# Summing messages by source: one-hots made one group ahead, and two turns in one PSUM bank

## The chip, the cores and the metric

The kernel runs on one core of a Trainium2 chip. The metric is device time in microseconds (us), from the start of the program to its end. The core has five engines with queues of their own: TensorE (PE, with its weight loads as PEld), VectorE (DVE), ScalarE (ACT), GpSimd (POOL) and SyncE (SP, which here only issues DMA transfers). An instruction starts when its turn in its engine's queue comes and the semaphores that it waits for have been raised.

## The reference

The kernel computes two graph layers and two mixture-of-experts layers on 6250 nodes with 256 features and 100000 edges. Only the first graph layer's sum matters here:

```python
row, col = (edge_index[0], edge_index[1])          # source and target of each edge
deg = segment_sum(ew_sl, row_sl, num_segments=N)
dinv = jnp.where(deg > 0, rsqrt(deg), 0.0)
norm = dinv[row_sl] * ew_sl * dinv[col_sl]
xw = h6_all @ W
msgs = xw[col_sl] * norm[:, None]
h7 = segment_sum(msgs, row_sl, num_segments=N) + b
h = relu(h7 @ W1 + b1)
out = h @ W2 + b2
```

`segment_sum` adds each edge's message to the row of its source node. After it come the two-layer head, a router over 8 experts (top 2), the experts, a second graph layer with 8 relations, and a second expert layer.

## The kernel before, in words

The nodes are held in 49 blocks of 128. A *turn* is a tile of 128 messages that all belong to one block; there are 830 turns (T), padded to 832 (TL), and they are taken in 104 groups of 8.

Before the stage in question, the messages stage (L848 to L935) has made each edge's message with a one-hot matmul (`pxn`, L908), scaled it on ACT (`msgn`, L923) and scattered it by an indirect DMA into the DRAM tensor `msgs`, in order of source. In that stage two message tiles already share one PSUM bank (L905, L906). Each row of `msgs` carries 256 values and the source number.

`sum_messages` (L944 to L972) then does, for each group:

- L948: the block numbers of the 8 turns are read into DVE registers;
- L949, L950: one load of 1 MB, `g`, is issued on SP; the tile has 4 buffers;
- L952: DVE makes `key`, from which each message's row in its block follows;
- L953 to L966: the 8 one-hot matrices `m` (2 buffers) are made: turns 0 and 1 by one DVE instruction (L954), turns 2 and 3 by two ACT instructions each (`far`, L963, then L964), turns 4 to 7 by POOL (L966);
- L967 to L972: for each turn one matmul (f32, which shows as two passes with a weight load each) writes `ps`, half of a PSUM bank, and DVE adds it to the block's place in the accumulator `acc` in SBUF (L971). The place is known only at run time, so each addition has a small register instruction in front of it. `psum_mm` (L67) hands out banks from a pool of 4.

`sum_messages` is a generator. `sum_and_send` (L1254) drives it. After each turn it may take one step of `send_group` (L1136), which for blocks whose sum is complete runs the head (`pt_h7`, `pg2`), the normalisation, the router (`pl1`, the small DVE steps of `route` and `top`) and the scatter of the rows to the experts (`xs`, L1243, on POOL). It also issues eight loads of `fw1` (L1274).

The order in which each engine takes its instructions is not the program's. The framework's scheduler decides it when the kernel is built, places the semaphore waits, and moves instructions that are ready ahead of others; `tc.keep_in_program_order` pins an instruction behind those that the program has before it on its engine. In the kernel before, the scheduler places `key` some three groups ahead of the additions of its group, and `m`'s DVE part one to two groups ahead.

The kernel is built with two versions of the stage, tags `l` and `e`; with these inputs the one tagged `e` runs, and the profile shows its tiles as `g0e`, `m0e`, `pa0e`.

Of the kernel before, what the change touches and what calls it, by code (L numbers as in the profile page):

```python
# [17 lines left out]
ENG = mybir.EngineType  # L18

N = 6250  # L20
D = 256
E = 100000
NT = 49
# [5 lines left out]
T = C_ + NT - 1  # L29
TL = (T + 7) // 8 * 8  # L30
# [27 lines left out]
def gnn_ffn_kernel(ctx: ExitStack, tc: tile.TileContext, a, out):  # L58
    nc = tc.nc
# [7 lines left out]
    def psum_mm(name):  # L67
        return p_mm.tile([128, 512], F32, tag="mm", name=name)
# [81 lines left out]
    col0, n = {}, 0  # L150
# [25 lines left out]
    def blocks_of(blk, t0, engines, top):  # L176
        _, v = nc.values_load_multi_w_load_instructions(
            blk[0:1, t0 : t0 + 8],
            engines=engines,
            min_val=0,  # L180
            max_val=top,
            skip_runtime_bounds_check_because="it is counted or bounded",
        )
        return v
# [176 lines left out]
    with tc.If(unsorted > 0):  # L361
        with tc.tile_pool(name="reorder", bufs=1) as rp:
# [49 lines left out]
            for q in range(QN):  # L412
                n = min(128, C_ - q * 128)
# [52 lines left out]
    for q0 in range(0, QN, 4):  # L466
        n = min(4, QN - q0)
# [53 lines left out]
    for b in range(NT):  # L521
        for h in range(2):
# [4 lines left out]
                start=(b == 0),  # L527
                stop=(b == NT - 1),
# [124 lines left out]
    for c0 in range(0, TN, DCH):  # L653
# [21 lines left out]
        for c in range(DCH):  # L675
# [4 lines left out]
                start=(c0 + c == 0),  # L680
                stop=(c0 + c == TN - 1),
# [30 lines left out]
    for t in range(NT):  # L712
        here = acc[:, t * D : (t + 1) * D]
# [15 lines left out]
    blks = g0p.tile([1, TL], I32, name="blks")  # L729
    firsts = g0p.tile([128, TL], F32, name="firsts")  # L730
# [212 lines left out]

    def sum_messages(pool, tag):  # L944

        for t0 in range(0, TL, 8):
            n = min(8, T - t0)
            blocks = blocks_of(blks, t0, [ENG.DVE], NT)  # L948
            g = pool.tile([128, 8, RW], F32, name=f"g0{tag}_{t0}", tag="g", bufs=4)  # L949
            nc.sync.dma_start(g, by_tile[:, t0 : t0 + 8, :])  # L950
            key = pool.tile([128, 8], F32, name=f"key{tag}{t0}", tag="key")
            nc.vector.tensor_sub(key[:, :n], firsts[:, t0 : t0 + n], g[:, :n, D])  # L952
            m = pool.tile([128, 8, 128], F32, name=f"m0{tag}_{t0}", tag="m", bufs=2)  # L953
            nc.vector.tensor_tensor(  # L954
                m[:, :2],
                minus[:, None, :].to_broadcast([128, 2, 128]),
                key[:, :2, None].to_broadcast([128, 2, 128]),
                OP.is_equal,
            )
            for j in range(2, n):  # L960
                if j < 4:
                    far = pool.tile([128, 128], F32, name=f"far{tag}{t0}_{j}", tag="far", bufs=2)
                    nc.scalar.activation(far, lanes, AF.Abs, bias=key[:, j : j + 1])  # L963
                    nc.scalar.activation(m[:, j], far, AF.Relu, bias=ones[:, 0:1], scale=-1.0)  # L964
                else:
                    nc.gpsimd.tensor_scalar(m[:, j], minus, key[:, j : j + 1], None, op0=OP.is_equal)  # L966
            for j in range(n):  # L967
                ps = psum_mm(f"pa0{tag}_{t0 + j}")
                nc.tensor.matmul(ps[:, :D], m[:, j, :], g[:, j, :D], start=True, stop=True)  # L969
                here = acc[:, bass.ds(blocks[j] * D, D)]  # L970
                nc.vector.tensor_add(here, here, ps[:, :D])  # L971
                yield t0 + j + 1  # L972

    def aggregate(pool, acc, table, tag):
# [279 lines left out]
    def sum_and_send(tag, early):  # L1254


        with (
            tc.tile_pool(name=f"sum{tag}", bufs=3, side="right") as sump,
            tc.tile_pool(name=f"mlp{tag}", bufs=1) as mlp,
        ):  # L1260
            seen, steps, waiting = [], None, list(GROUPS)

            def step(through):
                nonlocal steps
                if steps is None and waiting and through(sum(waiting[0])):
                    g, n = waiting.pop(0)
                    steps = send_group(g, n, mlp, tag, seen)
                if steps is not None and next(steps, steps) is steps:
                    steps = None

            for turn in sum_messages(sump, tag):
                if turn % 8 == 0 and 5 <= turn // 8 < 13:
                    e = turn // 8 - 5
                    nc.sync.dma_start(fw1[:, e], a["L0_ffn_w1"][e].rearrange("(k p) f -> p k f", p=128))  # L1274
                if early:
                    step(lambda blocks: S_TURNS * blocks + S_SLACK <= turn)
            while steps is not None or waiting:
                step(lambda blocks: True)
# [185 lines left out]
    def rows_in(t, i, stats):  # L1464

        xn = work.tile([128, D], F32, name=f"xn2_{t}", tag="xn", bufs=3)
        normed_in(xn, t, i, stats)
        xT = work.tile([128, 2, 128], F32, name=f"xT2_{t}", tag="xT")
        transpose_to(f"x2_{t}", xT, xn)
        return xT  # L1470
# [5 lines left out]
    ready = {0: rows_in(0, 0, stats[0])}  # L1476
    for gi, t, i in tiles:
# [12 lines left out]
        for r in range(0, NR, 2):  # L1490
            ps = psum_mm(f"phx{t}_{r}")
            for k in range(2):
# [4 lines left out]
                    start=(k == 0),  # L1497
                    stop=(k == 1),
# [11 lines left out]
        ps = psum_mm(f"plo{t}")  # L1510
# [219 lines left out]
```

## Time and profile before

| | |
|---|---|
| median of 3 runs | 4390.7 us (4375.65 to 4398.58) |
| the profiled execution's own time | 4087.26 us |
| its span | 4085.5 us |
| mean granted TensorE clock | 0.926 of full |
| PE, DVE, ACT, POOL busy | 85%, 50%, 32%, 55% of the span |
| matmuls of `pa0e` (L969), 2 passes a turn | 1344.7 to 2046.2 us |
| additions (L971) | 830, 0.42 us each |
| matmul rows of L969 | 1660, 501.7 us busy in all |
| POOL's one-hots (L966) | 414 of 0.64 us on the mean |
| ACT's one-hots (L964), second step | 208 of 0.40 us |
| DVE's one-hots (L954) | 104 of 0.42 us |

The profile is of one execution. A row of a group gives its source line, engine, operation, what it writes and reads (`out<-in`), how often, the busy time, the mean of one, and how long the engine stood idle just before and for whom. A row of the timeline gives start, length, engine, line and operation, and in brackets the idle time before it and the instruction whose end ended it. A row of the table by stretches gives the busy time and number of instructions of each engine. "Granted clock" is the share of full speed that TensorE was allowed.

### The profile page before, as it was taken

Reading aid. Unit: us, or ns where it says so; the run is one execution under the profiler, and the core shown is the slowest. Engines: PE = TensorE matmul, PEld = TensorE weight load, DVE = VectorE, ACT = ScalarE, POOL = GpSimd, SP = SyncE. Lnnn points to the kernel's source line nnn. Section 1 sums busy time; section 2 is a strip of 40 time slices with the busy share of each in tenths; the row PEclk is TensorE's granted clock in tenths of the full one; section 3 lists DMA queues with packets and bytes.
Section 4 is the critical chain, followed back from the end, with each engine's and each line's share of the span. In section 5 each row is a group of like instructions: output and inputs, shape, how many; then the busy total and the mean of one; then the engine's idle time right before and its main releaser. Section 6 shows DMA issues by size and latency. Waiting matters only on the chain.

```text
span 4085.5 us, 53140 instructions
## 1 busy us (share of the span) xinstructions
PE 3465.1 (85%) x14649; PEld 2311.2 (57%) x14649; DVE 2036.3 (50%) x5609; ACT 1325.1 (32%) x3006; POOL 2263.1 (55%) x2450
## 2 busy tenths in 40 slices
PE   7968877777776568888879968997789999999999
PEld 5756665665655345555557623443456666666656
DVE  6872111111111347778843387664556666666562
ACT  3714333333333113333334434663112222222213
POOL 1007777777777235555530086334767777777740
PEclk9989889989898679999989989997789999999999
DMA  4434333333333435555543345446555555555530
GB/s 120 168 112 161 128 126 126 129 128 129 127 128 122 150 112 199 198 199 195 182 154 108 99 166 195 197 197 226 151 141 152 154 150 155 150 151 150 148 110 9
DMA packets 227433, 602.86 MB, mean 148 GB/s; under 512 B 40620, under 2 KB 121689, under 8 KB 207276
## 3 DMA queue, kind: packets, MB, share of 16 engines
q0 software_dynamic: 100736, 295.11, 23.2%
q1 hardware_dynamic: 108242, 287.41, 20.9%
q10 hardware_dynamic: 18138, 16.68, 1.2%
q8 instruction: 131, 2.15, 0.2%
q14 instruction: 186, 1.52, 0.1%
HBM read 362.97 MB, written 236.11 MB: 147 GB/s over the span
## 4 chain that ended last, share of the span: by engine, by line
PE 37%; DVE 10%; issue 4%; DMA 2%; ACT 2%; POOL 2%; DVEq 0%; ACTq 0%; POOLq 0%; SPq 0%
PE ph_e1a L246 6%; PE py1a L1075 6%; PE pa1a L996 6%; PE ph_e2a L246 5%; PE phx L1493 4%; PE pf L1412 2%; PE pf L1428 2%; DVE rest L1503 2%; PE pa0e L969 2%; DVE acc L971 1%; DVE acc L1000 1%; DVE hx L1487 1%; PE pt_fh L234 1%; PE pcb1a L1595 1%; PE pqa L1567 1%
## 5 line engine op out<-in xcount | busy, mean ns | idle before, releaser
L988 POOL DMA_INDIRECT g1a<-hx,idxT x830 | 825.1, 994 | 321.0 <-PE pa1a L996 142.9
L908 PE MATMUL pxn<-acc,sTn 128*128 x3128 | 795.2, 415 | 243.4 <-DVE sTn L891 240.5
L926 POOL DMA_INDIRECT msgs<-msgn,at x782 | 785.4, 1004 | 271.0 <-DMA msgs<-msgn,at 122.8
L908 PEld LDWEIGHTS pxn<-acc,sTn 128*128 128x128 f32 x3128 | 618.5, 207 | 419.2 <-DVE sTn L891 272.3
L969 PE MATMUL pa0e<-g0e,m0e 128*128 128x256 f32 x1660 | 501.7, 436 | 156.2 <-DVE acc L971 70.8
L923 ACT ACTIVATE msgn<-pxn,ewT 128x256 f32<-128x256 f32 x782 | 370.2, 473 | 649.9 <-PE pxn L908 495.7
L1000 DVE TENSOR_TENSOR acc<-acc,pa1a 128x256 f32 x830 | 346.5, 417 | 341.2 <-PE pa1a L996 310.9
L969 PEld LDWEIGHTS pa0e<-g0e,m0e 128*128 128x128 f32 x1660 | 292.8, 206 | 328.7 <-issue 127.8
L966 POOL TENSOR_SCALAR m0e<-minus,keye 128x128 f32<-128x128 f32 x414 | 260.0, 642 | 318.8 <-PE pa0e L969 274.8
L899 DVE COPY msgn<-srcT 128x32 f32<-128x32 f32 x98 | 17.9, 185 | 829.6 <-DMA msgs<-msgn,at 666.7
L996 PE MATMUL pa1a<-g1a,m1a 128*128 128x256 bf16 x2490 | 375.5, 283 | 51.4 <-DMA g1a<-hx,idxT 36.1
L996 PEld LDWEIGHTS <-m1a 128*128 128x128 bf16 x2490 | 243.8, 100 | 275.8 <-issue 193.5
L1493 PE MATMUL phx<-wr,xT 128*128 128x512 f32 x784 | 370.1, 616 | 28.6 <-DVE rest L1503 20.8
L971 DVE TENSOR_TENSOR acc<-acc,pa0e 128x256 f32 x830 | 347.1, 418 | 94.7 <-PE pa0e L969 44.8
L1075 PE MATMUL py1a<-w_L_ffn_expert_w,v2a 128*128 128x256 f32 x1176 | 286.5, 384 | 6.0 <-DVE acc L1000 3.0
L246 PE MATMUL ph_e1a<-xT3a,w_L_ffn_expert_w 128*128 128x512 f32 (+2 forms) x672 | 288.5, 556 | 0.0
L246 PE MATMUL ph_e2a<-v1a,w_L_ffn_expert_w 128*128 128x512 f32 (+2 forms) x672 | 280.1, 542 | 2.1 <-DVE acc L1000 1.3
L253 ACT ACTIVATE v1a<-ph_e1a,cols 128x512 f32<-128x512 f32 (+2 forms) x168 | 106.5, 634 | 539.0 <-PE ph_e1a L246 532.0
L1493 PEld LDWEIGHTS phx<-wr,xT 128*128 128x128 f32 x784 | 148.0, 197 | 189.3 <-issue 163.7
L1453 POOL DMA_INDIRECT y<-ys,ats x98 | 97.3, 993 | 275.9 <-issue 261.1
L1075 PEld LDWEIGHTS py1a<-w_L_ffn_expert_w,v2a 128*128 128x128 f32 x1176 | 208.7, 190 | 44.1 <-ACT v2a L253 10.1
L1076 DVE SCALAR_TENSOR_TENSOR X<-py1a,C1a,X 128x256 f32<-128x256 f32 x294 | 138.8, 480 | 112.4 <-PE py1a L1075 111.4
(649 smaller groups left out, 4330.3 us busy)
## 6 DMA issues: line engine op xcount, KB each, us to landing
g0e<-msgs SPq DMA_DIRECT2D x104, 1040.0 KB
hx<-hx SPq DMA_DIRECT2D x49, 1536.0 KB
rowsn<-lane_rows SPq DMA_DIRECT2D x98, 256.0 KB
fx<-xs SPq DMA_DIRECT2D x105, 128.0 KB
ys<-fy ACTq DMA_DIRECT2D x105, 128.0 KB
g1a<-hx,idxT POOLq DMA_INDIRECT x830
msgs<-msgn,at POOLq DMA_INDIRECT x782
msgs<-none SPq DMA_DIRECT2D x10, 650.0 KB
```

Of the source, the lines that this page charges most:

```text
L246: nc.tensor.matmul(ps[:, :ncols], w[:, k, f * 128 : (f + 1) * 128], xT[:, k, :ncols], start=(k == 0), stop=(k == 1),)
L908: nc.tensor.matmul(come, sT[:, k, j, :], acc[:, bass.ds(blocks[j] * D + k * D, D)], start=(k == 0), stop=(k == 1),)
L923: nc.scalar.activation(msg[:, j, :D], come, AF.Copy, scale=ewT[:, t0 + j : t0 + j + 1])
L926: ins = nc.gpsimd.indirect_dma_start(out=msgs, out_offset=bass.IndirectOffsetOnAxis(ap=at[:, t0 + j : t0 + j + 1], axis=0), in_=msg[:, j, ...
L966: nc.gpsimd.tensor_scalar(m[:, j], minus, key[:, j : j + 1], None, op0=OP.is_equal)
L969: nc.tensor.matmul(ps[:, :D], m[:, j, :], g[:, j, :D], start=True, stop=True)
L971: nc.vector.tensor_add(here, here, ps[:, :D])
L988: nc.gpsimd.indirect_dma_start(out=g, out_offset=None, in_=table, in_offset=bass.IndirectOffsetOnAxis(ap=idxT[:, t0 + j : t0 + j + 1], axi ...
L996: nc.tensor.matmul(ps[:, :D], m[:, j, :], g[:, k * D : (k + 1) * D], start=(k == 0), stop=(k == 2))
L1000: nc.vector.tensor_add(here, here, ps[:, :D])
L1075: nc.tensor.matmul(ps[:, :D], hT[:, k, j : j + 128], w[:, k, :], start=(k == 0), stop=(k == 1))
L1493: nc.tensor.matmul(ps, xT[:, k, :], wr[:, k, r : r + 2, :].rearrange("p r o -> p (r o)"), start=(k == 0), stop=(k == 1),)
```

## The change

Three things change in `sum_messages`; nothing else does.

The loads are issued by `take`, three groups before the loop and then one for the group three ahead, at the top of each turn of the loop. The key and the one-hots of a group are made by `one_hots`, which is called once before the loop for group 0, and then inside the loop after the second addition (j == 1) of each group, for the next group. The subtraction that makes the key is pinned with `keep_in_program_order`, so it can't be moved ahead of that second addition on DVE; the one-hots read the key. Third, two neighbouring turns write the two halves of one bank: `pair` is taken for even j, and `ps` is its left or right half.

```diff
-        for t0 in range(0, TL, 8):
-            n = min(8, T - t0)
-            blocks = blocks_of(blks, t0, [ENG.DVE], NT)
+        def take(t0):
             g = pool.tile([128, 8, RW], F32, name=f"g0{tag}_{t0}", tag="g", bufs=4)
             nc.sync.dma_start(g, by_tile[:, t0 : t0 + 8, :])
+            return g
+
+        def one_hots(t0, g):
+            n = min(8, T - t0)
             key = pool.tile([128, 8], F32, name=f"key{tag}{t0}", tag="key")
-            nc.vector.tensor_sub(key[:, :n], firsts[:, t0 : t0 + n], g[:, :n, D])
+            tc.keep_in_program_order(nc.vector.tensor_sub(key[:, :n], firsts[:, t0 : t0 + n], g[:, :n, D]))
             m = pool.tile([128, 8, 128], F32, name=f"m0{tag}_{t0}", tag="m", bufs=2)
...
+            return m
+
+        come = {t0: take(t0) for t0 in (0, 8, 16)}
+        ready = one_hots(0, come[0])
+        for t0 in range(0, TL, 8):
+            n = min(8, T - t0)
+            blocks = blocks_of(blks, t0, [ENG.DVE], NT)
+            if t0 + 24 < TL:
+                come[t0 + 24] = take(t0 + 24)
+            g, m = come.pop(t0), ready
             for j in range(n):
-                ps = psum_mm(f"pa0{tag}_{t0 + j}")
-                nc.tensor.matmul(ps[:, :D], m[:, j, :], g[:, j, :D], start=True, stop=True)
+                if j % 2 == 0:
+                    pair = psum_mm(f"pa0{tag}_{t0 + j}")
+                ps = pair[:, j % 2 * D : (j % 2 + 1) * D]
+                nc.tensor.matmul(ps, m[:, j, :], g[:, j, :D], start=True, stop=True)
                 here = acc[:, bass.ds(blocks[j] * D, D)]
-                nc.vector.tensor_add(here, here, ps[:, :D])
+                nc.vector.tensor_add(here, here, ps)
+                if j == 1 and t0 + 8 < TL:
+                    ready = one_hots(t0 + 8, come[t0 + 8])
                 yield t0 + j + 1
```

Below, "a" and "b" are the first and the second turn of a pair, that is the left and the right half of a bank.

## The prediction

> **What bounds the kernel now.** I read the busy table by slices first (it says where TensorE is busy and at what clock), then the page's row of L969, then the waits inside that stage, then single instructions. The change touches only the sums by source (L944 to L972), which run from the first matmul of `pa0e` at 1344.7 us to the end of the last addition at 2048.2 us: 703.5 us of the span of 4085.5. The split by stretches:
>
> ```profile
> 1344.00:1543.00 199.00, 131.61 (x391) 88.35 (x391) 88.59 (x283) 37.73 (x112) 61.08 (x92) 0.76 0.38 132
> 1543.00:2048.00 505.00, 441.17 (x1854) 290.28 (x1853) 399.54 (x1526) 171.41 (x505) 285.67 (x410) 0.97 0.58 193
> ```
>
> Columns: length, then busy us of PE, PE's weight loads, DVE, ACT and POOL, then the granted clock, DMA share, GB/s. There are two regimes. The additions' own rows by stretch count 158 turns in the first 199 us (1.26 us a turn, 10.1 us for a group of 8) and leave 672 for the other 505 us (0.75 a turn, 6.0 a group). What DVE waits for over the whole stage (total us, times, longest):
>
> ```profile
> DVE keye L952 <- DMA g0e<-msgs: 72.9, 22, 8.5
> DVE acc L971 <- PE pa0e L969: 44.8, 74, 4.0
> DVE m0e L954 <- PE pa0e L969: 33.6, 23, 2.6
> ```
>
> 67.9 of the 72.9 us fall in the first stretch. A key sits in DVE's queue three groups ahead of its additions, so it waits for a load whose buffer only just came free, and the additions behind it wait too:
>
> ```profile
> 1391.27 0.17 DVE L952 TENSOR_TENSOR keye<-firsts,g0e 128x8 f32<-128x8 f32 x1 [3.59 <-DMA g0e<-msgs]
> 1391.44 0.42 DVE L971 TENSOR_TENSOR acc<-acc,pa0e 128x256 f32 x1
> 1391.97 0.30 PEld L969 LDWEIGHTS pa0e<-g0e,m0e 128*128 128x128 f32 x2 [3.87 <-issue]
> 1392.00 0.67 PE L969 MATMUL pa0e<-g0e,m0e 128*128 128x256 f32 x2 [3.50 <-DVE acc L971]
> 1392.36 2.52 DVE L971 TENSOR_TENSOR acc<-acc,pa0e 128x256 f32 x5 [0.50 <-DVE acc L971]
> ```
>
> In the second stretch those waits are gone. Additions follow each other every 0.52 us (five in 2.52), and small DVE steps of the sending hide in the 0.1 us between two. Hardly any slack is left: DVE and PE are each busy about 80 to 87%, and four banks let PE run four turns ahead.
>
> **What the change does, part by part.**
>
> *Keys and loads.* Each key now stands after the second addition of a group, for the next group, and its load was issued three groups ahead. A load lands about 4.9 us after issue (1386.40 to the key at 1391.27) and has some 15 us. The DMA wait goes: at most 72.9 us. SP's order of loads stays.
>
> *One-hots.* `m` uses buffers freed a group earlier, so DVE's 33.6 us of waiting for them goes. In the built order the DVE one-hot stands before the next addition in 22 groups (22 x 0.42 = 9 us on the path), and in a gap that exists anyway in the other 82. ACT's four steps take about 1.4 us (two pairs of 0.69) and POOL's 2.56, against a need about 2 and 4 us after the key: hidden, unless POOL's scatters (about 1 us each) stand ahead. Without that cover a late one-hot blocks all of PE's queue; 22.6 us of such waits are in the second stretch now, and I leave them.
>
> *Two turns in one bank.* This decides. In the built order of the changed kernel PE no longer does turns in sequence. In a quiet group it does (31.0b is the second half of group 31's pair 0)
>
> ```
> PE   31.0b 31.1b 32.0a 32.1a 31.2b 32.2a 31.3b 32.3a 32.0b ...
> DVE  load-of-blocks 31.0a 31.0b KEY 31.1a M 31.1b 31.2a 31.2b 31.3a 31.3b load-of-blocks 32.0a ...
> ```
>
> and every b matmul carries a wait on DVE that nothing but the addition of its own first half explains: already 0.0b has it, when all banks are fresh and its one-hot was there for 0.0a. DVE stays a, b, a, b. So after each first addition DVE stands until PE has filled the other half. The before trace has this hand-off with nothing in between:
>
> ```profile
> 1615.10 0.41 DVE L971 TENSOR_TENSOR acc<-acc,pa0e 128x256 f32 x1
> ...
> 1615.63 0.30 PEld L969 LDWEIGHTS pa0e<-g0e,m0e 128*128 128x128 f32 x2 [0.49 <-issue]
> 1615.66 0.67 PE L969 MATMUL pa0e<-g0e,m0e 128*128 128x256 f32 x2 [0.23 <-DVE seene L1215]
> ...
> 1616.33 0.42 DVE L971 TENSOR_TENSOR acc<-acc,pa0e 128x256 f32 x1 [0.65 <-DVE placee L1229]
> ```
>
> Addition ends 1615.51, weights start 1615.63 (0.12), the waiting addition starts 1616.33 (0.70). A pair's round is therefore 0.12 + 0.70 + 0.42 (b added) + 0.10 + 0.42 (next a added) = 1.76 us, against two turns at 0.75 = 1.50 now. The a half that PE does meanwhile starts 0.12 after b's addition and streams 0.43: it is out of the way by 0.58, the next b is due at 0.64. At full clock it hides with 0.06 to spare. Behind a waiting b in PE's queue stand the next a and, where sending runs, its transposes (ACT's copies wait for them); behind the waiting addition on DVE stand all later additions, the next key (ACT and POOL wait for it) and the sending's steps. One lost round is so lost for all.
>
> Does sharing a bank cost at all? The Trainium skill, "PSUM — Partial Sum Buffer", section "PSUM bank collisions raise a hardware error", says no two engines may touch one bank in the same partitions at once, so the guard has to be by bank and not by address, and its summary table sends a matmul beside a reader to a different bank. That speaks against this change. The nearest row speaks for it: the messages stage already shares banks so (L905):
>
> ```profile
> 1002.57 0.47 ACT L923 ACTIVATE msgn<-pxn,ewT 128x256 f32<-128x256 f32 x1 [0.39 <-PE pxn L908]
> 1003.43 0.47 ACT L923 ACTIVATE msgn<-pxn,ewT 128x256 f32<-128x256 f32 x1 [0.39 <-PE pxn L908]
> ```
>
> One read each 0.86 us, the reader idle half of it, PE never stopped. By that row sharing costs 0, and the stage would fall to DVE's own 8 x 0.52 + 0.4 + about 1 of sending = 5.6 us a group. But there four passes stand behind each read (0.86 us) and the reader is the idle side; here two passes (0.43) stand behind an addition every 0.52, and the adder's strict a, b order leaves nothing to do meanwhile. I take the rule, priced by the hand-off.
>
> *Load of the block numbers.* It costs DVE a gap of 0.50 instead of 0.10 (the 0.50 above). It is there now; on the new path it stays: 104 x 0.4 = 42 us.
>
> *Sending.* The small work between the turns is unchanged, but its cover changes. By the built order 540 of its DVE steps fall between a and b, into the 0.82 us wait. 240 fall between b and a; of these 50 are long (0.40 to 0.44, about 17 us net), the rest mostly fit the 0.1 us (10 us), and twelve overfull gaps add 6. Of its matmuls a quarter stand after an a half and delay a b: 18 of 0.43, 78 of about 0.2 = 23, with some overfull gaps 30. Together 63; DVE's and PE's parts overlap, so I take 40. Ends: 0 (all covered) and 100 (long waits for PE in line).
>
> *Clock.* At half clock a pass takes 0.42 (ten matmuls in 4.08 at 1392.93) instead of 0.215; b and the a in front of it then both lengthen the round: b 0.43 later, a 0.35 beyond its cover, 0.8 us a pair. "TensorE: Matmul & The Clock Gate", section "HAM oscillation", ties the drop to idle gaps over about 3.4 us; the new loop has none over 0.8, so by the rule 0. By rows, the table stage at 2420 to 2470 us, 69% busy with short gaps, was granted 0.88, which is a quarter of the time at half: 0.24 x 0.8 x 415 = 80 us. The new loop would show two rows of 0.67 in 1.76, 76%. Between the two I take 0.95: 30 us.
>
> *Sum.* 415 x 1.76 = 730, + 42 + 9 + 40 + 30 = 851 us for the stage, against 703: +148. All removed waits (72.9 + 33.6 + 44.8) are already in this, since the stage is built anew. By stretch, in groups of 851/104 = 8.2 us, the first 20 groups gain about 35 us and the other 84 lose about 184. Nothing after the stage starts otherwise.
>
> The profiled execution took 4087.26 us (span 4085.5), the median of the runs is 4390.7; the trace doesn't show what these 303 us are. Added unchanged: 4390.7 + 148 = 4539, rounded 4540. Scaled by 4390.7/4087.26 it would be 4550.
>
> **The rivals.**
> 1. *It does what it says* (faster, other side). Place: DVE between a and b. If that wait vanishes or shrinks, the DMA and one-hot waits are gained and nothing is paid: 104 x 5.6 = 582, −121, so 4270. It decides from a pair's round of about 1.43 us downward ((703 − 42 − 9 − 40 − 20) / 415). For: the messages rows. Against: 1.76 is made of measured parts, and the waits are in the build. 0.06.
> 2. *Gain and loss cancel*: round 1.5, within noise. 0.03.
> 3. *Bare loop*: sending and clock hidden, 730 + 42 + 9 = 781, +78, so 4469. For: gaps of 0.82 in every pair. 0.20.
> 4. *Forecast*, 4490 to 4585. 0.54.
> 5. *Loop with a falling clock*: granted 0.80 instead of 0.95 gives 0.4 x 0.8 x 415 = 133 instead of 30, +251, so 4642. For: 0.76 in the first stretch, whose PE rows are 66% busy. Against: its gaps of 3.5 us. 0.17.
>
> **Numbers.** Time 4540. Range from just under the bare loop to near the slow clock, 4455 to 4635. Faster 0.06, within 0.5% (about 22 us, what a measurement of this kernel can tell from no change) 0.03, slower 0.91.
>
> **What would show it.** After: no wait of `keye` for DMA; additions in twos, 0.10 apart inside "b, next a", then about 0.8 us of waiting for PE; DVE waiting for PE in `pa0e` rising from 44.8 to over 250 us; 7.5 us for a quiet group; clock 0.9 to 1.0; stage about 850 us. I'm wrong if additions come every 0.52 again (rival 1), or if the granted clock falls below 0.85 (rival 5), or if PE stands for POOL's one-hots for more than 30 us.

## The result and the profile after

| | before | after |
|---|---|---|
| median of the runs | 4394.64 us (4 runs, 4375.65 to 4409.77) | 4628.4 us (4 runs, 4594.83 to 4644.64) |
| ratio, 95% interval | | 1.0524 [1.0452, 1.0597] |
| profiled execution, span | 4085.5 us | 4623.2 us |
| sums by source, first matmul to last addition | 703.5 us | 946.2 us (1469.6 to 2415.8) |
| span outside the stage | 3382 us | 3677 us |
| granted TensorE clock, whole span | 0.926 | 0.887 |

The change costs 234 us by the medians, 5.2%. The forecast was 4540, with 4455 to 4635 as its range. The spans of the two traces can't be subtracted: before took 4385 to 4395 us in three sets of runs and 4086 in a fourth, which ran on a chip of its own, and its profile is from the lower level, that of after from the upper. The difference lies outside the stage, where the profiles of the upper level have 3677 to 3695 us and those of the lower 3382 to 3393, whatever was changed in the stage; its cause was not looked for. So the stage is compared here, and each ratio is against before in the same set of runs. The stage grew by 243 us, which is the whole loss within the spread of the runs.

The stage of after by stretches (first the length, then for PE, weight loads, DVE, ACT and POOL the busy us and in brackets the number of instructions, then granted clock, DMA share, GB/s):

```profile
1469.00:1600.00 131.00, 96.06 (x249) 56.58 (x250) 52.42 (x157) 23.87 (x70) 32.94 (x52) 0.64 0.38 135
1600.00:1800.00 200.00, 149.14 (x438) 90.86 (x438) 104.48 (x378) 38.99 (x119) 74.06 (x108) 0.70 0.37 124
1800.00:2000.00 200.00, 142.35 (x521) 88.20 (x520) 117.83 (x431) 47.28 (x143) 78.58 (x116) 0.88 0.41 140
2000.00:2200.00 200.00, 140.68 (x535) 86.10 (x534) 122.84 (x441) 48.77 (x147) 77.04 (x116) 0.93 0.41 139
2200.00:2416.00 216.00, 161.98 (x522) 100.00 (x521) 119.84 (x426) 47.35 (x143) 73.72 (x110) 0.76 0.34 117
```

Neither PE nor DVE is near its limit any more: over the stage DVE is busy 517 us of 947, and the clock is 0.79 on the mean. The waits of DVE in the stage (total us, times, longest):

```profile
DVE acc L987 <- PE pa0e L985: 345.2, 313, 8.0
...
DVE keye L956 <- DMA g0e<-msgs: 8.4, 1, 8.4
```

and of PE:

```profile
PE pa0e L985 <- DVE acc L987: 99.0, 172, 1.5
PE pa0e L985 <- ACT fare L967: 67.5, 50, 15.4
PE pa0e L985 <- POOL m0e L970: 30.7, 8, 6.1
```

The key's wait for its load is gone but for the first one, and DVE's wait for free `m` buffers is no longer in the list. In their place additions wait 345 us for matmuls and matmuls 99 us for additions: two engines, each waiting for the other. What one round looks like, DVE at full clock:

```profile
1882.36 0.88 DVE L987 TENSOR_TENSOR acc<-acc,pa0e 128x256 f32 x2 [0.39 <-PE pa0e L985]
1884.07 0.42 DVE L987 TENSOR_TENSOR acc<-acc,pa0e 128x256 f32 x1 [0.83 <-PE pa0e L985]
```

Two additions back to back (a pair's second half and the next pair's first), then 0.83 us of standing: 1.71 us from pair to pair. The same loop at half clock, DVE and then PE:

```profile
1699.99 0.88 DVE L987 TENSOR_TENSOR acc<-acc,pa0e 128x256 f32 x2 [1.04 <-PE pa0e L985]
1702.64 0.88 DVE L987 TENSOR_TENSOR acc<-acc,pa0e 128x256 f32 x2 [1.77 <-PE pa0e L985]
```

```profile
1703.20 2.04 PE L985 MATMUL pa0e<-g0e,m0e 128*128 128x256 f32 x4 [0.60 <-DVE acc L987]
```

Now the round takes 2.65 us. PE starts 0.56 after the row of two additions does, that is 0.14 after the first of them ends; it does a later a and then the b that is due, four passes in 2.04, and the addition starts as they end. At full clock the a is hidden; at half clock it is on the path. Quiet groups (those without sending) show the two clocks as sharply: between two keys lie 7.20 us at full clock (three rounds of about 1.71 and one of 2.05 with the load of the block numbers) and 10.20 at half. In the first groups, before any sending, it is about 7.7 and 11.2. Hardly any quiet group lies between.

### The profile page after: what moved, and what is told of

It is laid out like the page before. It is cut to its first block, busy times and chain, and to the rows that moved or that the text cites. A ratio compares the mean times of both kernels' runs of the same rounds, so it can differ in the third digit from the quotient of the medians.

```text
span 4623.2 us, 52530 instructions
## 1 busy us (share of the span) xinstructions
PE 3664.8 (79%) x14649; PEld 2386.5 (52%) x14649; DVE 2090.5 (45%) x5609; ACT 1315.9 (28%) x3006; POOL 2247.8 (49%) x2450
## 4 chain that ended last, share of the span: by engine, by line
PE 59%; DVE 13%; issue 12%; POOL 6%; ACT 3%; another core or an unknown queue 3%; DMA 2%; DVEq 1%; SPq 0%; ACTq 0%; POOLq 0%
PE pxn L908 11%; PE pa0e L985 11%; PE pa1a L1014 6%; PE ph_e1a L246 6%; PE py1a L1093 5%; PE ph_e2a L246 5%; POOL msgs L926 4%; PE phx L1511 4%; DVE acc L987 3%; PE pf L1430 2%; PE pf L1446 2%; DVE rest L1521 1%; DVE we L664 1%; DVE ohl L656 1%
## 5 line engine op out<-in xcount | busy, mean ns | idle before, releaser
L908 PE MATMUL pxn<-acc,sTn 128*128 x3128 | 841.5, 429 | 338.6 <-ACT msgn L923 198.7
L908 PEld LDWEIGHTS pxn<-acc,sTn 128*128 128x128 f32 x3128 | 642.3, 215 | 535.4 <-ACT msgn L923 234.2
L985 PE MATMUL pa0e<-g0e,m0e 128*128 128x256 f32 x1660 | 609.1, 495 | 260.0 <-DVE acc L987 99.0
L985 PEld LDWEIGHTS pa0e<-g0e,m0e 128*128 128x128 f32 x1660 | 337.1, 235 | 502.4 <-issue 186.0
L970 POOL TENSOR_SCALAR m0e<-minus,keye 128x128 f32<-128x128 f32 x414 | 249.8, 620 | 567.1 <-DVE keye L956 426.2
L891 DVE TENSOR_SCALAR sTn<-rowsn,far_parts 128x1024 f32<-128x1024 bf16 x196 | 142.8, 768 | 537.0 <-PE pxn L908 471.5
L1093 PE MATMUL py1a<-w_L_ffn_expert_w,v2a 128*128 128x256 f32 x1176 | 296.8, 391 | 31.3 <-issue 13.0
L967 ACT ACTIVATE fare<-lanes,keye 128x128 f32<-128x128 f32 x208 | 72.8, 394 | 630.6 <-DVE keye L956 589.6
```

The costliest lines, as they stand in the source:

```text
L908: nc.tensor.matmul(come, sT[:, k, j, :], acc[:, bass.ds(blocks[j] * D + k * D, D)], start=(k == 0), stop=(k == 1),)
L985: nc.tensor.matmul(ps, m[:, j, :], g[:, j, :D], start=True, stop=True)
L1093: nc.tensor.matmul(ps[:, :D], hT[:, k, j : j + 128], w[:, k, :], start=(k == 0), stop=(k == 1))
```

## The experiments

The theory: the guard of a bank makes each b matmul wait for the addition of its own a, and the two hand-offs of that wait are the new bound. There are three rivals: first, the loss comes from the pinned keys and late one-hots (ACT, POOL); second, from a bank's two halves being written and read close together, in whatever order; third, from the clock alone.

**Own banks.** The new one-hots stay, each turn has a bank of its own.

```diff
-                if j % 2 == 0:
-                    pair = psum_mm(f"pa0{tag}_{t0 + j}")
-                ps = pair[:, j % 2 * D : (j % 2 + 1) * D]
+                ps = psum_mm(f"pa0{tag}_{t0 + j}")[:, :D]
```

> The change without its shared banks: every turn takes a bank of its own again; loads, keys and one-hots stay one group ahead and pinned. If the shared bank is the cost (my theory), the additions come every 0.52 us again, a group takes about 5.6 us, the stage about 580 to 620 us against 703 before and 946 after, the granted clock in it over 0.95, and the ratio to before is 0.96 to 0.98. If instead the pinned, later one-hots are the cost (rival: TensorE stands for ScalarE's and GpSimd's one-hots, 98 us after), the stage stays over 800 us and the ratio over 1.02.

Measured: 0.9872 [0.9844, 0.9899], 4328.66 us against 4384.82. The stage, its waits of DVE and of PE:

```profile
1477.00:2126.00 649.00, 546.44 (x2242) 365.77 (x2241) 485.81 (x1806) 203.50 (x615) 338.25 (x501) 0.94 0.56 190
```

```profile
DVE acc L985 <- PE pa0e L983: 98.3, 113, 6.0
...
PE pa0e L983 <- POOL m0e L970: 51.5, 30, 7.0
```

The stage is 649 us long, 297 less than with shared banks and about 55 less than before's. The clock is back at 0.94. So the pinned keys and one-hots are a gain by themselves, and the first rival falls, although PE waits more for POOL (51.5 us) than in after (30.7). The gain is smaller than expected (649 us in place of 580 to 620). The third rival falls too: a quiet group takes about 5.0 us here and 7.20 in after at full clock, which by estimate is 229 of the 297 us (104 groups at 2.2). Run once more on another chip it gave 0.9897 [0.9852, 0.9942].

> The kernel with a bank for every turn once more, on this chip: 0.982 to 0.992 of before.

**Pairs only.** The other half of the change alone: before's keys and one-hots, with `pair` and `ps` as in after.

> The kernel before with nothing but the shared banks; keys and one-hots where the scheduler put them before. Shared bank as the cost: rounds of 1.7 us at full and 2.65 us at half clock here too, stage 900 to 1000 us, ratio 1.045 to 1.07. One-hots as the cost: stage about 703 us, ratio within 0.01 of 1.

Measured: 1.077 [1.0741, 1.08], 4724.28 us. Stage 1040 us, clock 0.54 in its first 227 us and 0.73 later:

```profile
DVE acc L973 <- PE pa0e L971: 432.9, 319, 7.1
DVE keye L952 <- DMA g0e<-msgs: 28.2, 17, 2.1
```

Shared banks alone cost 337 us over before's 703, more than expected, and the clock is lower still than in after. So they carry the whole loss, and the pinned one-hots, 55 us to the good alone, make it smaller with shared banks too (946 against 1040).

**Both matmuls first.** The same two turns share the same bank, but both halves are written before either is read.

```diff
                 if j % 2 == 0:
                     pair = psum_mm(f"pa0{tag}_{t0 + j}")
+                    for i in range(j, min(j + 2, n)):
+                        nc.tensor.matmul(
+                            pair[:, i % 2 * D : (i % 2 + 1) * D], m[:, i, :], g[:, i, :D], start=True, stop=True
+                        )
                 ps = pair[:, j % 2 * D : (j % 2 + 1) * D]
-                nc.tensor.matmul(ps, m[:, j, :], g[:, j, :D], start=True, stop=True)
```

> The changed kernel with both matmuls of a pair written ahead of its two additions; the same banks are shared. If the cost is that the second half waits for the first half's addition (my theory), it is gone though the bank is shared: stage 570 to 620 us, ratio 0.96 to 0.98. If sharing a bank between a writer and a reader is slow in itself, or the one-hots are the cost, the stage stays over 800 us and the ratio over 1.02.

Measured: 0.9866 [0.9844, 0.9888], 4327.86 us, stage 646 us, clock 0.93; once more, 0.9888 [0.9858, 0.9917].

> The kernel with both matmuls first once more, on this chip: 0.982 to 0.992 of before, within 0.3% of the one with a bank for every turn, since DVE (additions, loads of block numbers, one-hots and the sending, some 600 of 645 us) limits both.

The stage was expected at 570 to 620 us, but the cost of sharing is gone: it is free here when the order is write, write, read, read. The second rival falls with that, since the two halves are still written and read close together. A row of DVE in this order:

```profile
1706.10 2.37 DVE L990 TENSOR_TENSOR acc<-acc,pa0e 128x256 f32 x5
```

Five additions stand in one row of 2.37 us: no wait inside or between pairs.

**Sharers four turns apart.** Turns j and j + 4 share a bank, so that a's reader is long done when b is due.

```diff
+            banks = [None] * 4
...
-                if j % 2 == 0:
-                    pair = psum_mm(f"pa0{tag}_{t0 + j}")
-                ps = pair[:, j % 2 * D : (j % 2 + 1) * D]
+                if j < 4:
+                    banks[j] = psum_mm(f"pa0{tag}_{t0 + j}")
+                ps = banks[j % 4][:, j // 4 * D : (j // 4 + 1) * D]
```

> The changed kernel with turns j and j+4 of a group in one bank instead of j and j+1. The second half still waits for the addition of the first half, but that lies four turns back. If only the neighbourhood is the cost: additions every 0.52 us in most places, stage 580 to 660 us, ratio 0.96 to 0.99. If any sharing costs a hand-off per half, the stage is 850 us or more, ratio over 1.03.

Measured: 0.992 [0.9891, 0.9948], 4349.35 us, stage 662 us, clock 0.94. All but 13 us of the 297 are back, though each bank is still written, read, written and read. So what costs is a's reader coming close ahead of b's writer, not the shared bank.

**Both first, before's one-hots.**

> The kernel before (keys and one-hots where its scheduler put them), with two turns in a bank and both matmuls of a pair ahead of both additions. If only the order around the shared bank costs, this is no slower than before: ratio 0.98 to 1.01, and what separates it from the changed kernel with both matmuls first (0.9866) is the worth of the one-hots' new place. If the new place is worth nothing, it equals that one within 0.3%.

Measured: 0.9876 [0.9859, 0.9892], 4035.52 us against 4086.0, stage 644 us. The keys still wait for their loads:

```profile
DVE keye L952 <- DMA g0e<-msgs: 62.4, 24, 8.6
```

Two matmuls at a time on one bank give as much over before as the pinned one-hots do, and the two together no more: the stages are 644 us here, 646 with both and 649 with own banks and pinned one-hots. DVE is busy 478 to 486 us of each. Where this kernel's gain comes from was not tested: DVE's waits for PE's additions and for free `m` buffers are shorter than before (32.7 and 17.4 us, where they were 44.8 and 33.6), and four banks now hold eight turns in place of four.

**Own banks, without the pin.** As own banks, and the key's subtraction is written without `keep_in_program_order` (the part of the edit that differs from own banks):

```diff
-            tc.keep_in_program_order(nc.vector.tensor_sub(key[:, :n], firsts[:, t0 : t0 + n], g[:, :n, D]))
+            nc.vector.tensor_sub(key[:, :n], firsts[:, t0 : t0 + n], g[:, :n, D])
```

> The changed kernel with a bank for every turn (ratio 0.9872) and without the pin on the key. The scheduler then moves keys up by several additions. If the pin is what takes the wait for the loads away, DVE waits for loads again, 20 us or more, and the ratio is 0.99 to 1.0; if the earlier issue of the loads and the place in the program do it alone, 0.985 to 0.989, or lower, since GpSimd gets its keys sooner.

Measured: 1.0003 [0.9994, 1.0012], 4086.62 us, stage 699:

```profile
DVE keye L956 <- DMA g0e<-msgs: 65.7, 23, 5.2
DVE acc L985 <- PE pa0e L983: 42.8, 71, 4.0
DVE m0e L958 <- PE pa0e L983: 33.3, 23, 2.6
```

These are before's three waits again, almost to the number (this window leaves out the first key's wait of 8.7 us, which before's 72.9 and the 62.4 above include). Writing the calls in another place changes nothing; the pin does it all.

**More one-hots on ACT.** Both first, and ACT makes those of turns 4 and 5 too.

```diff
-                if j < 4:
+                if j < 6:
```

> Both matmuls first, and one-hots 4 and 5 of each group moved from GpSimd to ScalarE, which is idle most of the stage. GpSimd's late one-hots made TensorE wait 78 us there, in 11 waits behind a burst of eight scatters. If these waits are the next limit, the stage falls from 646 to about 600 us and the ratio from 0.987 to about 0.977; if ScalarE's longer chain (four more steps of 0.35 us) then comes late, 0.985 to 1.0.

Measured: 0.987 [0.9853, 0.9886], 4032.48 us, stage 641: no more than both first alone, where about 600 was expected. POOL's busy time fell from 338 to 218 us, yet PE waits for POOL's one-hots 73.7 us in 11 places, where it was 78.5 in 11. There are 11 bursts of eight scatters, and the waits are for those, not for POOL's total. How POOL's scatters hold up its one-hots, from after:

```profile
2204.14 0.97 POOL L1261 DMA_INDIRECT xs<-toke,ats  x1 [0.30 <-issue]
2205.13 2.36 POOL L970 TENSOR_SCALAR m0e<-minus,keye 128x128 f32<-128x128 f32 x4
```

```profile
2205.83 1.22 PE L985 MATMUL pa0e<-g0e,m0e 128*128 128x256 f32 x4 [2.28 <-POOL m0e L970]
```

The last of eight scatters, each 1.28 us after the other; POOL's one-hots start only behind it, and PE has stood for 2.28 us.

**More work for PE.** If the clock falls because PE has too little to do in the loop, more matmuls should bring it back. In the first kernel the whole first matmul of each pair is done twice, in the second its left 128 columns are:

```diff
+                if j % 2 == 0:
+                    nc.tensor.matmul(ps, m[:, j, :], g[:, j, :D], start=True, stop=True)
                 nc.tensor.matmul(ps, m[:, j, :], g[:, j, :D], start=True, stop=True)
```

```diff
+                if j % 2 == 0:
+                    nc.tensor.matmul(ps[:, :128], m[:, j, :], g[:, j, :128], start=True, stop=True)
                 nc.tensor.matmul(ps, m[:, j, :], g[:, j, :D], start=True, stop=True)
```

> The changed kernel with the first matmul of each pair done twice in a row (415 matmuls more, the same result). If the granted clock falls because TensorE streams only about half of a round (0.86 of 1.71 us), the third matmul raises the streaming share to about 0.6: the clock in the stage rises from 0.79 to over 0.9, a round takes about 2.1 us instead of a mix of 1.71 and 2.65, and the stage takes 900 to 1000 us against 946, ratio to before 1.04 to 1.07. If the clock doesn't depend on how busy TensorE is, the quiet groups stay at half clock and every pair pays 0.4 to 0.9 us more: stage 1100 to 1300 us, ratio 1.09 to 1.13.

> The changed kernel with half of the first matmul of each pair (128 of its 256 columns) done once more. It lengthens a round at full clock by at most 0.15 us (62 us in all) and raises TensorE's streaming share of a round from 0.50 to about 0.58. If too little streaming is what halves the clock: quiet groups of 7.2 to 7.8 us throughout, clock in the stage over 0.9, stage 840 to 910 us, so 1 to 2.5% faster than the changed kernel although it does more. If the clock isn't decided by that: quiet groups up to 11 us still, 0 to 2% slower than the changed kernel.

> The changed kernel itself, for a comparison on one chip with the next three. Between its 1.0524 and 1.0623, the ratio with every first matmul done twice: 1.050 to 1.062. Quiet groups of 7.2 us at full clock and 10.2 us at half clock, mixed, in other places than before.

Measured: whole matmul twice 1.0623 [1.0605, 1.0641], stage 946 us; left half twice 1.0538 [1.0505, 1.0571], stage 936; after itself, again, 1.0551 [1.051, 1.0592], stage 928. The stage of the second kernel:

```profile
1478.00:1600.00 122.00, 89.08 (x380) 61.33 (x380) 58.84 (x192) 25.23 (x74) 35.18 (x56) 0.93 0.42 150
1600.00:1800.00 200.00, 153.35 (x674) 109.25 (x674) 114.42 (x401) 43.92 (x134) 78.67 (x116) 0.91 0.40 136
```

Where after was granted 0.64 and 0.70, this kernel with half a matmul more in a pair is granted 0.93 and 0.91; over the stage it is 0.90, and 0.94 in the first kernel. The quiet groups of the second kernel are 7.65 us but for two of 11.83 at half clock, which follow waits of PE for POOL of 3.30 and 5.72 us; those of the first are 7.73, none at half clock. The early groups of the second took 8.16, where after's took 11.18. That the clock answers to PE's work is shown. But the total did not fall as expected: the second kernel's stage was to take 840 to 910 us, and the whole took as long as after beside it (4625 us both). The longer round and the groups with sending and scatters (up to 16 us, and 17.7 in the first kernel, against 14.5 in after) took back what the clock gave. In after run again the later half-clock groups lay in other places: 0.91 was granted from 1600 to 1800 us, where it had 0.70, and 0.82 from 2000 to 2200, where it had 0.93.

## Why the prediction was right, and where it was not

The forecast was right in its direction, in the step that decides and in its range, but the time lies only 7 us inside the range's upper end, and two terms of the sum were too small.

*Two turns in one bank* held, and decides. The round was put at 1.76 us and measured 1.71; without the shared bank's order (both first) it is gone, with it alone (pairs only) it is all there. DVE's wait for PE was to pass 250 us and is 345.

*The rule against the row.* I took the Trainium skill's guard by bank ("PSUM — Partial Sum Buffer", section "PSUM bank collisions raise a hardware error") against the messages stage's row, in which sharing costs nothing. The runs bear the guard out where the chain is: PE waits 99 us for additions in after and 8.6 with own banks, and both first and sharers four turns apart show that it costs next to nothing where b's matmul need not come straight behind a's reader. Why the messages stage pays nothing was not tested; its program also writes and reads the halves in turn, and the reason that I gave there, matmuls of 0.86 us beside each read of 0.47, is only argued.

*Keys, loads and one-hots* held as a mechanism: the DMA wait fell from 72.9 to 8.4, and own banks shows what this part is worth, 55 us. The 35 us that the early groups were to gain did not come in after: in its first 199 us it made 151 additions, where before made 157, since those groups ran at half clock (11.18 us each).

*Load of the block numbers, quiet group*: the round with the load took 0.34 more, put at 0.4; a quiet group 7.20, put at 7.5. The DVE one-hot hides in the quiet groups.

*The sum.* 104 quiet groups of 7.20 are 749 us, where rounds and loads were put at 772. The other 197 us of the stage are sending and clock, where 70 (and 9 for the one-hot) were put. That is where the 95 us between 851 and 946 come from. To part the two: in the second run of after, 46 groups in a row (1639.75 to 2026.09) were granted 0.92 and took 8.40 us each. At that pace the stage is 873 us, so half clock costs some 73 us of after's 946, if those groups, which hold some half clock themselves, stand for the rest. The granted 0.79 means half clock for 0.42 of the stage, 397 us; at 0.94 lost in each 2.65 that is 141, if every lost microsecond were on the path. So the clock took about 73 to 141, put at 30; sending the remaining 56 to 124, put at 40. Both terms were too small.

*The clock* is the step that failed as a step, in three places. The rule weighed there ("TensorE: Matmul & The Clock Gate", section "HAM oscillation") ties the drop to idle gaps over about 3.4 us, and I took the term by it as 0, since no gap was to pass 0.8. But the waits for POOL's one-hots that I left aside as 22.6 us are such gaps: before has them up to 4.4 us, after seven of 3.31 to 6.08 (three of them just under the rule's length), and rows at half clock stand behind each of these seven. Then, the clock also fell without such a gap, and stayed at half for seven groups on end (11.0 to 11.2 us each) in which PE's gaps were 0.60 and 1.15 us. Last, I misread the row of the table stage: five of its gaps are 1.8 to 4.1 us long, and behind one of 2.85 eight passes take 5.37 us where the next eight take 3.60:

```profile
2450.62 5.37 PE L1493 MATMUL phx<-wr,xT 128*128 128x512 f32 x8 [2.85 <-DVE rest L1503]
...
2456.05 3.60 PE L1493 MATMUL phx<-wr,xT 128*128 128x512 f32 x8
```

That row's 80 us lie inside what was measured by luck. Granted 0.79 is rival 5's case: with its own formula, 0.42 x 0.8 x 415 = 139 in place of 30, the sum is 960, and the stage took 946. So the likeliest case was wrong in the clock, and the rival that was given 0.17 describes the run best.

*Sending*: the named cover (DVE waits of 0.82 us) hid the small steps, but not the bursts of scatters. Nine of the eleven groups with a burst take 11.4 to 14.5 us; in the second run of after the five among the 46 groups cost 25 us over the quiet 7.20, the half clock behind their waits included. PE stood 30.7 us for POOL's one-hots, just over the 30 that I had named as a bound.

Of the other rivals, *bare loop* fell with clock and sending, *it does what it says* and *gain and loss cancel* with the 0.83 us of waiting in every round.

Three things stay open: the exact parting of clock and sending, why the time outside the stage has two levels, and whether one-hots made two groups ahead would cover the bursts of scatters, which was not tried.

## What to carry over

If two tiles share a PSUM bank, write both before either is read, or put the sharers several turns apart; write, read, write, read on one bank in neighbouring turns chains two engines, and two additions that take 1.04 us back to back take 1.71. Costing such a chain from one isolated hand-off in the trace worked to 3%. A chain also thins the matmuls, so its time should be worked out at half clock as well, and that case weighed as heavily as the one at full clock; and waits that an estimate leaves aside should be held against the rule for the clock too. The kernels here with own banks and pinned one-hots, and those with both first and either kind of one-hots, were all 1.0 to 1.3% faster than before.

## What the runs showed of the hardware

The clock of after fell to half in the middle of a regular loop. PE's rows at that moment:

```profile
1485.46 1.10 PE L985 MATMUL pa0e<-g0e,m0e 128*128 128x256 f32 x4 [0.60 <-DVE acc L987]
1487.17 1.45 PE L985 MATMUL pa0e<-g0e,m0e 128*128 128x256 f32 x4 [0.61 <-DVE acc L987]
1489.77 1.94 PE L985 MATMUL pa0e<-g0e,m0e 128*128 128x256 f32 x4 [1.15 <-DVE m0e L958]
1492.31 2.04 PE L985 MATMUL pa0e<-g0e,m0e 128*128 128x256 f32 x4 [0.60 <-DVE acc L987]
```

and by stretches, with the granted clock as the third number from the right:

```profile
1485.00:1489.00 4.00, 2.47 (x8) 1.23 (x8) 1.92 (x6) 0.00 (x0) 0.00 (x0) 1.00 0.34 92
1489.00:1493.00 4.00, 2.62 (x6) 1.67 (x7) 1.76 (x6) 1.28 (x4) 2.57 (x4) 0.62 0.42 175
1500.00:1578.00 78.00, 57.42 (x115) 32.91 (x116) 26.86 (x73) 9.58 (x30) 18.03 (x28) 0.50 0.26 88
1578.00:1590.00 12.00, 9.78 (x39) 6.03 (x37) 8.62 (x34) 3.13 (x11) 2.34 (x4) 0.97 0.46 153
```

The gaps are the same before and after the fall, 0.60 us a pair and 1.15 a group, and the four passes go from 1.10 us to 2.04. The loop then stays at half for some 90 us, until the first matmuls of sending fill PE's gaps (from 1573.50), and is back at full clock soon after 1578. In the second run of after the first fall comes as late (22 us into the stage, against 20), and later ones lie elsewhere.

A long wait brings the clock down as well. In after, each of the seven waits for POOL's one-hots of 3.31 us or more has rows at half clock right behind it:

```profile
1855.52 1.10 PE L985 MATMUL pa0e<-g0e,m0e 128*128 128x256 f32 x4 [0.17 <-DVE acc L987]
1859.93 2.07 PE L985 MATMUL pa0e<-g0e,m0e 128*128 128x256 f32 x4 [3.31 <-POOL m0e L970]
```

Six of these stretches end within 4 to 10 us, one lasts 39. But four others, of 33 to 88 us and some 230 together, have no gap over 1.4 us right ahead of them.

Passes of 0.215 us fill 0.86 of the full-clock round of 1.71, half of it. With half a matmul more in each pair the gaps are as long (0.60 us a pair, 1.06 to 1.20 a group), yet the eight early groups ran at full clock, and where the clock fell, mostly behind waits for POOL, it was back within 25 us. So in this loop, gaps being equal, it was the share of streaming that decided whether and how long the clock stayed at half.
